# An adapter product moved behind a chunk's gate half, with its loads reordered, in an FFN kernel on one core

## Chip, cores and metric

The kernel runs on one core of a Trainium2 chip. The metric is the device time of one execution in microseconds (us). Before the change the median of four runs is 474.83 us, from 474.81 to 474.93.

A core has engines that run side by side, each with its own instruction stream: TensorE (PE in the profile, its weight loads PEld), VectorE (DVE), ScalarE (ACT), GpSimd (POOL) and SyncE (SP), which here only issues transfers. They wait for one another through semaphores.

## What is computed

Each of 8 batches of x (256 rows of 1024) goes through a low-rank adapter chosen by its id, then through a gated FFN whose activations are rounded to fp8, and is added to x:

```python
# x: (8, 256, 1024); per batch one adapter: B (16 x 1024), A (1024 x 16)
Bx  = einsum('bni,bri->bnr', x, B[ids])
c   = einsum('bnr,bor->bno', Bx, A[ids])
gate = fq(c) @ gate_w.T          # gate_w, up_w: (2752, 1024)
up   = fq(c) @ up_w.T            # fq: to fp8 and back, with a scale
hidden = silu(gate) * up
out  = x + fq(hidden) @ down_w.T # down_w: (1024, 2752)
```

## The kernel before

The 2048 tokens are four blocks t = 0..3 of 512, two batches each. Everything is held transposed, tokens along the free dimension. A block has three steps: B's product (`bx`, 64 small matmuls), A's product (`c`), whose result is rounded to fp8 into `xg[t]`, and the big products. The 2752 hidden rows are 22 chunks c of 128 (the last has 64). For a chunk and a block, `gate_up(c, t)` makes 16 matmuls of 128x512 into two PSUM tiles `y`: eight (k = 0..7) for the gate, j = 0, and eight for the up half, j = 1. ACT takes the silu (L702), DVE multiplies and rounds to `hid` (L731). After all chunks the down projection runs (`yd`) and the result goes out.

The first NFIRST = 5 chunks are held in SBUF, and the blocks enter one after another while their inputs still arrive: block 0 with chunks 0 to 4, block 1 with chunks 0 to 2, then chunks 3 and 4 of block 1 with the adapter products of blocks 2 and 3 between them. From chunk 5 on, all four blocks take each chunk (L780 to L785).

Block 1's adapter is the part in question. `block_1` (L765) is called between steps 11 and 12 of `gate_up(4, 0)`. It first writes DVE's half of the split of A (`split`, L448: two instructions, L454 and L455, that write into `a_parts[0]`, for A's rows held twice, the rounded value in the one copy and what rounding leaves over in the other; POOL does the other half of the columns at L473, as early as A has landed). Then `two_times_b_in_parts` (L585) issues the 64 matmuls on x's block 1 and B, and takes the result apart: a rounded part `bm_parts` (L597, one half by DVE, one by ACT), what is left, `rest` (L600, DVE), and a copy of each to the other partitions (L608, ACT). After the four matmuls that remain of chunk 4, `two_times_a_parts` (L659) makes c of the two halves of the columns: for each, 8 matmuls on bm_parts and 8 on rest, into four PSUM tiles, which ACT and DVE round to xg (L614, L616). Then `gate_up(0, 1)` begins.

PE's instructions are issued in the order in which they are written (`multiply`, L524), and so are the DVE and ACT instructions named above. A PSUM tile is one of eight slots that go round.

All loads of this stage are issued by SyncE in the order written, but for a few at the start that ACT issues. Each issue waits until the one eight places before has landed. The order is: x of block 0 in four pieces, with B and A for it between; chunks 0 (in two loads) to 4 (L422); the adapter numbers of six batches read into registers (L424); B for block 1 (two loads of 68 KB); x of block 1, k = 0..6 (L427, 1792 KB); A for block 1 (L431, four loads of 64 KB); x of block 1, k = 7 (L432, 256 KB); x of blocks 2 and 3 (2 MB each) and their B and A. A chunk is 1 MB, 128 rows of 16 blocks of 128; `gate_up_of` (L78) says where, and the host lays out the blocks of a chunk's row in the order h, j, k, where h is the upper or lower half of the eight k (L993). L718 picks the block for (j, k).

```python
        gate_up(NFIRST - 1, 0, between={12: block_1})
        two_times_a_parts(bms[0])
        gate_up(0, 1, turns=(2, 2, 2, 2))
```

With turns=(2, 2, 2, 2), the gate and the up half take turns by two k, so that the first steps need only the first columns of xg.

Of the kernel before, what the change touches and what calls it, by code (L numbers as in the profile page):

```python
# [19 lines left out]
P = 128  # L20
# [6 lines left out]
NH = H // P  # L27
NI = (I + P - 1) // P
# [5 lines left out]
NFIRST = 5  # L34
# [3 lines left out]
KS = NH // 2  # L38
# [9 lines left out]
def rows_of(c):  # L48
    return TAIL if c == NI - 1 else P


def high(ap):

    return ap.bitcast(BF16)[..., 1::2]
# [6 lines left out]
def x_of(x4, t, k):  # L61

    first = 0
    for n in PIECES[t]:
        if k < first + n:
            break
        first += n
    at = (t * NH + first) * P * TB
    piece = x4[at : at + n * P * TB].rearrange("(p k n) -> p k n", p=P, k=n)
    return piece, first  # L70


def x_row(x4, t, k):
    piece, first = x_of(x4, t, k)
    return piece[:, k - first, :]


def gate_up_of(w_gu, c):  # L78
    at = c * 2 * NH * P * P
    return w_gu[at : at + 2 * NH * P * rows_of(c)].rearrange("(p n) -> p n", p=P)  # L80
# [13 lines left out]
def general(  # L94
# [62 lines left out]
    def three_parts(w):  # L157
        parts = [w]
        rows, size = w.shape[0], prod(w.shape[1:])
        for i in range(2):  # L160
            r = shaped(wpool.tile([P, 2 * NH * P], F32, tag=f"r{i}", name=f"g_r{i}"), w)
            nc.vector.tensor_tensor(r, parts[-1], high(parts[-1]), ALU.subtract)
            parts.append(r)
        return parts
# [29 lines left out]
    def gate_up(hid):  # L194
        for c in range(NI):
            n = rows_of(c)
            w = wpool.tile([P, 2 * NH * P], F32, tag="w", name="g_wgu")
            nc.sync.dma_start(out=w[:, : 2 * NH * n], in_=gate_up_of(w_gu, c))
            w = w[:, : 2 * NH * n]

            order = "p (h j k n) -> p h j k n" if n == P else "p (h k j n) -> p h j k n"
            ws = [
                high(part).rearrange(order, h=2, j=2, k=KS) for part in three_parts(w)
            ]
            ps = []
            for j, x in enumerate((xg, xu)):
                y = psum.tile([P, TB], F32, tag="ps", name=f"g_y{j}")[:n]
                terms = [(k, part) for part in ws for k in range(NH)]
                for i, (k, part) in enumerate(terms):
                    nc.tensor.matmul(  # L210
                        y,
                        lhsT=part[:, k // KS, j, k % KS, :],
                        rhs=x[:, k, :],
                        start=(i == 0),
                        stop=(i == len(terms) - 1),
                    )
                ps.append(y)
            g = work.tile([P, TB], F32, tag="g", name="g_g")[:n]
            nc.scalar.activation(g, ps[0], AF.Silu, scale=gate_s[:n])
            v = work.tile([P, TB], F32, tag="v", name="g_v")  # L220
            nc.vector.scalar_tensor_tensor(
                v[:n],
                in0=ps[1],
                scalar=up_by_down[:n],
                in1=g,
                op0=ALU.mult,
                op1=ALU.mult,
            )
            quantize(hid[:n, c, :], v, n)
# [55 lines left out]
def adaln_ffn(  # L285
# [64 lines left out]
    with ExitStack() as fast:  # L350
# [23 lines left out]
        def adapter_of(batch, queue):  # L374
            return queue.value_load(ids_i[0:1, batch : batch + 1], min_val=0, max_val=7)  # L375
# [6 lines left out]
        def load_a_two(t, j, adapter, queue=nc.sync):  # L382
            for g in range(2):
                row = 32 * (2 * g + j) + R * j
                queue.dma_start(
                    out=a_two[t][row : row + R],
                    in_=a8[bass.ds(adapter * 2 * R + g * R, R), :],
                )
# [6 lines left out]
        def load_x(t, k):  # L395
            piece, first = x_of(x4, t, k)
            ks = slice(first, first + piece.shape[1])
            nc.sync.dma_start(out=xs[t][:, ks, :], in_=piece)  # L398

        w_of = {}  # L400

        def load_gate_up(c, parts=1):
            n = NH if c == NI - 1 else 2 * NH
            w = wpool.tile([P, 2 * NH, P], F32, tag="w", name="w_gu")[:, :n]
            src = gate_up_of(w_gu, c).rearrange("p (k n) -> p k n", n=P)
            n //= parts
            for i in range(parts):
                nc.sync.dma_start(out=w[:, bass.ts(i, n)], in_=src[:, bass.ts(i, n)])
            w_of[c] = w

# [6 lines left out]
        load_a_two(0, 0, first, nc.scalar)  # L419
        load_x(0, 7)  # L420
        load_a_two(0, 1, second, nc.sync)
        for c in range(NFIRST):  # L422
            load_gate_up(c, parts=1 if c else 2)
        adapters = [adapter_of(2 + q, nc.sync) for q in range(6)]  # L424
        for j in range(2):
            load_b(b_two[1], j, adapters[j], nc.sync)
        load_x(1, 0)  # L427
        for j in range(2):
            adapter = adapters.pop(0)
            for g in range(2):  # L430
                load_a_twice(a_two[1], 2 * g + j, a8_twice, adapter * 2 + g)  # L431
        load_x(1, 7)  # L432

        for t in (2, 3):
            load_x(t, 0)
# [12 lines left out]
        def split(a, parts, engine):  # L448

            held = tc.keep_in_program_order
            held(engine.tensor_scalar(parts, a, minus, None, ALU.mult))  # L454
            held(engine.tensor_tensor(parts, a, parts.bitcast(F32), ALU.add))  # L455
# [228 lines left out]
        def gate_up(c, t, turns=(NH,), between={}):  # L684


            tail = c == NI - 1
            w = w_of[c]
            cols = bass.ts(t, TB)
            js = range(1 if tail else 2)  # L690
            ys = []
            steps = []
            for i, n in enumerate(turns):
                done = sum(turns[:i])
                steps += product(js, range(done, done + n))
            rows = slice(TAIL, P) if tail else slice(0, P)
            g = work.tile([P, TB], F32, tag="g", name="g")

            def silu():
                gates = ys[0][:TAIL] if tail else ys[0]  # L700
                early(
                    nc.scalar.activation(  # L702
                        g[rows], gates, AF.Silu, scale=gate_s[: gates.shape[0]]
                    )
                )

            def early(instruction):
                if c < NFIRST:
                    tc.keep_in_program_order(instruction)

            for i, (j, k) in enumerate(steps):
                if i in between:
                    between[i]()
                if j == len(ys):
                    ys.append(psum.tile([P, TB], F32, tag="ps", name=f"y{j}"))
                multiply(
                    ys[j],
                    lhsT=high(w[:, k if tail else k // KS * NH + j * KS + k % KS, :]),  # L718
                    rhs=xg[t][:, k, :],
                    start=(k == 0),  # L720
                    stop=(k == NH - 1),
                )
                if j == 0 and k == NH - 1:
                    silu()
            ups = ys[0][TAIL:] if tail else ys[1]
            if tail:
                to = lora.tile([P, 2 * TB], FP8, tag="bm", name="tail", bufs=2)[half_of(t), :TB]
            else:
                to = hid_of(c)[:, cols]
            early(  # L730
                nc.vector.scalar_tensor_tensor(  # L731
                    to,
                    in0=ups,
                    scalar=up_by_down[rows],
                    in1=g[rows],
                    op0=ALU.mult,
                    op1=ALU.mult,
                    saturate=False,
                )
            )  # L740
            if tail:
                nc.vector.tensor_copy(hid_tail[half_of(t), t // 2], to)
            if t == (NTB - 1 if c < NFIRST else 1):
                note_low_bits(w_of[c], P, c)
                if 1 < c <= 1 + 2 * NTB:
                    i, half = divmod(c - 2, 2)
                    ks = slice(half * NH // 2, (half + 1) * NH // 2)
                    note_squares(xg[i][:, ks, :], P, c - 2)
                if c:
                    note_squares(hid[c - 1], P, 2 * NTB + c - 1)  # L750
# [12 lines left out]
        bms = []  # L763

        def block_1():  # L765
            split(a_two[1][:, : H // 4], a_parts[0][:, : H // 4], nc.vector)
            bms.append(two_times_b_in_parts())

        gate_up(NFIRST - 1, 0, between={12: block_1})
        two_times_a_parts(bms[0])  # L770
        gate_up(0, 1, turns=(2, 2, 2, 2))
        for c in range(1, NFIRST - 2):
# [138 lines left out]
    with found_others.Else():  # L911

        k = NH - 1
# [101 lines left out]
```

## Time and profile before

| what | value |
|---|---|
| median of 4 runs | 474.83 us (474.81 to 474.93) |
| the profiled execution | 474.79 us |
| its span in the trace | 473.0 us |
| granted PE clock in the span | 1.0 |
| y matmuls, 128x512 | 1376 |
| chain that ended last: y, yd, c, bx | 63%, 32%, 1%, 1% of the span |
| x for block 0 on that chain | 1% |
| DVE, hid of one chunk and block (L731) | 751 ns |
| DVE, xg (L614) / ACT, xg (L616) | 744 / 688 ns |
| w_gu loads of 1024 KB, median from issue to landing | 4.8 us |
| bytes moved in the span | 53.84 MB, mean 114 GB/s |

The span is what the profile shows of the core; the time of the execution is 1.8 us longer. A row of the timeline gives the start in us, the length in us, the engine, the line of the kernel, the operation, the tile written and the tiles read, the shapes, and how many instructions are merged. In brackets stands the idle time of the engine before it and who ended it. A queue's name with a q (SPq) is an issue of a transfer and not its duration. Matmuls are pipelined: a 128x512 matmul is shown as 379 ns, but the next one starts after 0.22 us.

### The profile page before, as it was taken

To read this page: it belongs to the slowest core of one execution; us is meant where nothing else is said; L and a number is where in the kernel's file an instruction comes from. 1 tells how busy PE (TensorE), PEld (TensorE's weight loads), DVE (VectorE), ACT (ScalarE), POOL (GpSimd) and SP (SyncE) were. 2 spreads that over 40 slices of the span, in tenths; PEclk is the share of its full clock that TensorE was granted. 3 is DMA by queue.
4 is the path that set the end of the run, shared out by engine and by line. 5 is a ranking of instruction groups with operands and counts; after the bars stand their busy time and mean duration, and the time that the engine had idled before them with its cause. 6 is when DMAs were issued, how large, how long until landed. Compare 5 with 4: busy or idle time off the path is not lost.

```text
span 473.0 us, 5972 instructions
## 1 busy us (share of the span) xinstructions
PE 468.3 (99%) x2482; PEld 215.7 (46%) x2482; DVE 106.9 (23%) x168; ACT 193.5 (41%) x252; POOL 11.6 (2%) x26
## 2 busy tenths in 40 slices
PE   8999999999999999999999999999999999999997
PEld 5454544444444444444444444444444444444444
DVE  1342611212121221212122121231120111031031
ACT  1341538996555645443354544359112012021000
POOL 0024200000000000000000000000000000000000
PEclk9999999999999999999999999999999999999999
DMA  8996024322222211222220011133435245153021
GB/s 319 419 387 202 1 91 139 129 89 89 90 89 90 78 25 76 89 90 89 90 73 31 30 62 57 61 101 106 128 123 161 73 178 162 37 207 108 4 114 69
DMA packets 13909, 53.84 MB, mean 114 GB/s; under 512 B 1650, under 2 KB 2930, under 8 KB 10930
## 3 DMA queue, kind: packets, MB, share of 16 engines
q1 hardware_dynamic: 13664, 53.25, 32.3%
q8 instruction: 21, 0.34, 0.3%
q10 hardware_dynamic: 210, 0.14, 0.1%
q14 instruction: 14, 0.11, 0.1%
HBM read 44.99 MB, written 8.39 MB: 113 GB/s over the span
## 4 chain that ended last, share of the span: by engine, by line
PE 97%; DMA 1%; SPq 0%; DVE 0%; issue 0%
PE y L525 63%; PE yd L525 32%; PE c L525 1%; PE bx L525 1%; DMA x<-x 1%; DMA ids_i<-ids 0%; DVE xg L614 0%; SPq L375 0%; PE warm L525 0%; SPq L398 0%; SPq L378 0%; DVE o L822 0%; PE count L525 0%
## 5 line engine op out<-in xcount | busy, mean ns | idle before, releaser
L525 PE MATMUL y<-xg,w_gu 128*128 128x512 fp8e4 x1376 | 298.1, 379 | 0.4 <-DVE xg L614 0.4
L525 PEld LDWEIGHTS <-w_gu 128*128 128x128 bf16 x1376 | 134.0, 98 | 162.7 <-issue 0.6
L525 PE MATMUL yd<-hid,w_d 128*128 128x512 fp8e4 (+2 forms) x693 | 146.0, 373 | 0.0
L702 ACT ACTIVATE g<-y,gate_s 128x512 f32<-128x512 f32 (+1 forms) x88 | 59.7, 682 | 141.1 <-PE y L525 141.0
L731 DVE SCALAR_TENSOR_TENSOR hid<-y,up_by_down,g 128x512 fp8e4<-128x512 f32 x84 | 63.1, 751 | 217.4 <-PE y L525 153.7
L525 PEld LDWEIGHTS <-w_d 128*128 128x128 bf16 x693 | 66.6, 98 | 78.9 <-issue 1.7
L511 ACT ACTIVATE junk<-w_d 128x1408 bf16<-128x1408 uint16 (+1 forms) x16 | 21.2, 1323 | 88.5 <-DMA w_d<-w_d 88.4
L822 DVE SCALAR_TENSOR_TENSOR o<-yd,down_s,x 128x512 f32<-128x512 f32 x28 | 20.0, 747 | 107.3 <-PE yd L525 95.1
L511 ACT ACTIVATE junk<-w_gu 128x2048 bf16<-128x2048 uint16 (+1 forms) x22 | 41.0, 1863 | 0.0
L518 ACT ACTIVATE junk<-hid 128x2048 bf16<-128x2048 fp8e4 x21 | 40.0, 1906 | 0.5
L518 ACT ACTIVATE junk<-xg 128x2048 bf16<-128x2048 fp8e4 x8 | 15.3, 1910 | 0.3
L614 DVE TENSOR_SCALAR xg<-c,inv 128x512 fp8e4<-128x512 f32 x16 | 10.9, 744 | 4.7 <-PE c L525 4.7
L616 ACT ACTIVATE xg<-c,inv 128x512 fp8e4<-128x512 f32 x16 | 9.7, 688 | 1.7 <-PE c L525 1.7
L525 PE MATMUL warm<-zeros 128*128 128x512 bf16 (+1 forms) x27 | 6.5, 400 | 1.2 <-DVE zeros L312 1.2
L822 DVE SCALAR_TENSOR_TENSOR o<-yd,down_s,xg 128x512 f32<-128x512 f32 (+2 forms) x5 | 3.2, 644 | 12.4 <-PE yd L525 9.8
L525 PEld LDWEIGHTS <-zeros 128*128 128x128 bf16 x27 | 2.6, 116 | 4.6 <-issue 2.9
L511 ACT ACTIVATION_READ_ACCUMULATOR junk<-w_gu 128x1 f32 x22 | 4.2, 192 | 0.0
L525 PE MATMUL yd<-hid_tail,w_dt 64*128 64x512 bf16 (+1 forms) x32 | 4.2, 377 | 0.0
L731 DVE SCALAR_TENSOR_TENSOR tail<-y,up_by_down,g 64x512 fp8e4<-64x512 f32 x4 | 3.0, 756 | 4.9 <-ACT g L702 4.8
L518 ACT ACTIVATION_READ_ACCUMULATOR junk<-hid 128x1 f32 x21 | 3.9, 187 | 0.0
L525 PE MATMUL bx<-x,b_four_twice 128*32 128x256 f32 x64 | 3.7, 380 | 0.0
L578 ACT COPY bm<-bx 64x128 f32<-64x128 f32 x2 | 0.5, 262 | 7.1 <-PE bx L525 7.1
(69 smaller groups left out, 56.3 us busy)
## 6 DMA issues: line engine op xcount, KB each, us to landing
w_gu<-w_gu SPq DMA_DIRECT2D x20, 1024.0 KB, 4.8
outT<-o SPq DMA_DIRECT2D x31, 256.0 KB, 2.2
w_d<-w_d SPq DMA_DIRECT2D x8, 704.0 KB, 5.0
w_d<-w_d SPq DMA_DIRECT2D x8, 640.0 KB, 3.8
x<-x SPq DMA_DIRECT2D x2, 2048.0 KB, 12.2
x<-x SPq DMA_DIRECT2D x1, 1792.0 KB, 13.1
w_gu<-w_gu SPq DMA_DIRECT2D x3, 512.0 KB, 4.0
x<-x SPq DMA_DIRECT2D x2, 512.0 KB, 4.0
```

What stands on the lines that cost most here:

```text
L511: nc.scalar.activation(junk_like(w), low(w), AF.Copy, accum_out=lows[:rows, column : column + 1])
L518: nc.scalar.activation(junk_like(q), q, AF.Square, accum_out=squares[:rows, column : column + 1])
L525: tc.keep_in_program_order(nc.tensor.matmul(*args, **kwargs))
L578: copy(bm[64 * to : 64 * (to + 1), other], bx[half][64 * half : 64 * (half + 1)],)
L614: nc.vector.tensor_scalar(to, c, scale, None, ALU.mult, saturate=False)
L616: nc.scalar.activation(to, c, AF.Copy, scale=scale, saturate=False)
L702: nc.scalar.activation(g[rows], gates, AF.Silu, scale=gate_s[: gates.shape[0]])
L731: nc.vector.scalar_tensor_tensor(to, in0=ups, scalar=up_by_down[rows], in1=g[rows], op0=ALU.mult, op1=ALU.mult, saturate=False,)
L822: nc.vector.scalar_tensor_tensor(o, in0=y, scalar=down_s, in1=x, op0=ALU.mult, op1=ALU.add)
```

## The change

Block 1's product is issued between steps 7 and 8 of `gate_up(4, 0)`, that is between chunk 4's gate and its up half, and no longer after the fourth up matmul. In `block_1` DVE's half of A's split comes after the product's rounding and rests. Chunk 4 is laid out in the order j, h, k (all of the gate's blocks first) and loaded in two loads of 512 KB: the gate half at its old place, the up half (`ups_of_last`) behind x of block 1, whose last piece (k = 7) now follows the first directly. A for block 1 comes after the up half. The functions `order_of` and `row_of` carry the layout to the places that read chunk 4.

```diff
+def order_of(c):
+    return "h k j" if c == NI - 1 else "j h k" if c == NFIRST - 1 else "h j k"
+
+def row_of(c, j, k):
+    if c == NI - 1:
+        return k
+    return j * NH + k if c == NFIRST - 1 else k // KS * NH + j * KS + k % KS
...
-        def load_gate_up(c, parts=1):
+        def load_gate_up(c, parts=1, later=()):
...
+            w_of[c] = w
             n //= parts
-            for i in range(parts):
+
+            def load(i):
                 nc.sync.dma_start(out=w[:, bass.ts(i, n)], in_=src[:, bass.ts(i, n)])
-            w_of[c] = w
+
+            for i in range(parts - len(later)):
+                load(i)
+            return [lambda i=i: load(i) for i in later]
...
-        for c in range(NFIRST):
+        for c in range(NFIRST - 1):
             load_gate_up(c, parts=1 if c else 2)
+        ups_of_last = load_gate_up(NFIRST - 1, parts=2, later=(1,))
         adapters = [adapter_of(2 + q, nc.sync) for q in range(6)]
         for j in range(2):
             load_b(b_two[1], j, adapters[j], nc.sync)
-        load_x(1, 0)
+        for k in (0, 7):
+            load_x(1, k)
+        for load in ups_of_last:
+            load()
         for j in range(2):
             adapter = adapters.pop(0)
             for g in range(2):
                 load_a_twice(a_two[1], 2 * g + j, a8_twice, adapter * 2 + g)
-        load_x(1, 7)
...
-                    lhsT=high(w[:, k if tail else k // KS * NH + j * KS + k % KS, :]),
+                    lhsT=high(w[:, row_of(c, j, k), :]),
...
         def block_1():
+            bms.append(two_times_b_in_parts())
             split(a_two[1][:, : H // 4], a_parts[0][:, : H // 4], nc.vector)
-            bms.append(two_times_b_in_parts())
-
-        gate_up(NFIRST - 1, 0, between={12: block_1})
+
+        gate_up(NFIRST - 1, 0, between={8: block_1})
...
-                .transpose(0, 2, 1, 3, 4)
+                .transpose(0, *((1, 2) if c == NFIRST - 1 else (2, 1)), 3, 4)
```

More of the change, by code (lines that the diff above doesn't have):

```diff
@@ L199, in gate_up @@
             w = w[:, : 2 * NH * n]
-            order = "p (h j k n) -> p h j k n" if n == P else "p (h k j n) -> p h j k n"
+            order = f"p ({order_of(c)} n) -> p h j k n"
             ws = [
```

## The prediction

> **What bounds the kernel now.** First I read the page: who holds the chain that ends last, and how much of the span TensorE (PE) is busy.
>
> ```profile
> span 473.0 us, 5972 instructions
> PE 468.3 (99%) x2482; PEld 215.7 (46%) x2482; DVE 106.9 (23%) x168; ACT 193.5 (41%) x252; POOL 11.6 (2%) x26
> PE 97%; DMA 1%; SPq 0%; DVE 0%; issue 0%
> ```
>
> PE is busy for 468.3 of 473.0 us and holds 97% of the chain. The change adds and removes no matmul, so all it can give is idle PE time near the edit. The windows of 5 us show where that is: none from 10 to 30 us and none from 35 to 55 us, but 4.58 of 5.00 busy here:
>
> ```profile
> 30.00:35.00 5.00, 4.58 (x74) 2.69 (x65) 4.31 (x10) 3.41 (x9) 1.61 (x2) 1.00 1.01 410
> ```
>
> (The columns are PE, PEld, DVE, ACT and POOL busy, then the granted PE clock, 1.00, the DMA share and GB/s.) The timeline from 28 to 34.2 us shows what happens there; each row is start, length, engine, line:
>
> ```profile
> 28.87 1.96 PE L525 MATMUL bx<-x,b_twice 128*32 128x128 f32 x64
> 29.74 0.35 DVE L454 TENSOR_SCALAR a_parts<-a,minus 128x256 fp32r<-128x256 f32 x1 [2.52 <-DMA a<-a_twice]
> 29.82 1.07 POOL L454 TENSOR_SCALAR a_parts<-a,minus 128x256 fp32r<-128x256 f32 x1 [5.37 <-DMA a<-a_twice]
> 30.12 0.58 DVE L455 TENSOR_TENSOR a_parts<-a,a_parts 128x256 fp32r<-128x256 f32 x1
> 30.76 1.04 PE L525 MATMUL y<-xg,w_gu 128*128 128x512 fp8e4 x4
> 30.86 0.28 DVE L597 CAST bm_parts<-bx 64x128 fp32r<-64x128 f32 x1 [0.16 <-PE bx L525]
> 30.97 0.72 POOL L455 TENSOR_TENSOR a_parts<-a,a_parts 128x256 fp32r<-128x256 f32 x1
> 31.18 0.61 DVE L600 TENSOR_TENSOR rest<-bx,bm_parts 64x128 fp32r<-64x128 f32 x2
> 31.73 0.66 PE L525 MATMUL c<-bm_parts,a_parts 32*128 32x256 f32 x8
> 31.74 0.61 ACT L608 CAST rest<-rest 64x128 fp32r<-64x128 f32 x2
> 32.40 0.51 PE L525 MATMUL c<-rest,a_parts 32*128 32x256 f32 x8
> 32.97 1.41 DVE L614 TENSOR_SCALAR xg<-c,inv 128x512 fp8e4<-128x512 f32 x2 [0.39 <-PE c L525]
> 33.78 0.61 PE L525 MATMUL y<-xg,w_gu 128*128 128x512 fp8e4 x2 [0.40 <-DVE xg L614]
> ```
>
> The reader is to see a chain with too little behind it. B's product ends at 30.8. DVE and ACT turn it into a rounded part and a rest (until 32.35), and only four y matmuls (30.76 to 31.64) stand before A's product c. The c on bm_parts start at 31.73, those on rest only at 32.40. DVE's first xg follows at 32.97, and 0.81 later the next y, at 33.78. Last, SyncE's issues, which tell when the transfers land:
>
> ```profile
> 15.42 0.43 SPq L398 DMA_DIRECT2D x<-x  x1
> 16.06 4.88 SPq L391 DMA_DIRECT2D a<-a_twice  x4
> 23.18 0.83 SPq L398 DMA_DIRECT2D x<-x  x2
> ```
>
> The page's list of issues gives the 1792 KB piece of x 13.1 us to landing: 15.42 + 13.1 = 28.5. POOL and DVE start the split when A has landed, 29.7. The last 256 KB of x must be in by the product's k = 7, 28.87 + 56 x 0.0295 = 30.52, since its 64 matmuls run at an even step (1.89 us / 64).
>
> **The change part by part.** The sum is made in the profiled execution (474.79 us; span 473.0). The median of the runs shown, 474.83, is 0.04 above it.
>
> *B's product four y earlier.* A y step is 0.2185 us (16.64 us / 76). The product starts at 28.87 - 4 x 0.2185 = 28.00 and the following y at 30.76 - 0.87 = 29.89. PE's amount of work until c is unchanged, so without a stall c would again start at 31.73. What changes is the cover: eight y, 1.75 us, instead of four.
>
> *Rounding and rest.* DVE and ACT follow the product as before, 0.87 earlier: DVE's cast 29.99, its two rests 30.31 to 30.92, ACT's copies of the rest until 32.35 - 0.87 = 31.48. All of it lies behind the eight y. Before, the c on rest waited: behind c at 31.73 they could have started 0.34 later (the A product at 49.67 has its rest part at 50.01), 32.07, and started at 32.40. So 0.33 us is removed, and the shorter c phase may give some more, 0.44 in all (below).
>
> *Split behind the rests.* Its two DVE instructions cost 0.35 + 0.58 and 0.03 between them, 0.96 us. Before, they were done at 30.70 under the product. Now they run 30.94 to 31.90, if A is there. All c of the first half need them. DVE's end to PE's start takes 0.07 (the first xg, 0.744 long, ends at 33.71; y starts 33.78): c at 31.97 instead of 31.73. That gives 0.24 of the gain back. Bounds: not under 0.80 (0.35 plus 0.42, the L670 subtraction of 128x256 from PSUM, plus 0.03); above, it could stand until POOL's half of the split is through (priced in the rivals). I take 0.96, which is this very pair with POOL running beside it.
>
> What is queued behind the split on DVE: the hid of chunk 4, 31.92 to 32.67 instead of 31.84 to 32.59. Then xg, which must not start before 32.67; it has 0.10 to spare. A slot of the second half's c waits for that hid too, as before.
>
> *From c to the next y.* In the unstalled A product of blocks 2 and 3, c starts at 49.67 and DVE's first xg at 50.47: 0.80. Block 1's own rows give 32.97 - 31.73 - 0.33 = 0.91. I take 0.80, the same shapes without a stall: xg at 32.77, y at 32.77 + 0.81 = 33.58 instead of 33.78, a gain of 0.20 us (0.09 with 0.91).
>
> *Loads.* Chunk 4's up half (512 KB) goes behind x, A behind that. At 420 GB/s (the windows between 10 and 25 us show 419 to 428) 512 KB are 1.25 us and 256 KB 0.62. The order on SyncE's queue holds in the trace (chunk 4 in by about 23.2, B 23.4, x 28.5, A 29.7), so:
> - chunk 4's gate by about 21.9, needed at 12.30 + 64 x 0.2185 = 26.3. B for POOL's copies at 22.2 instead of 23.4.
> - x 27.25, needed 28.00; its last piece 27.9, needed 28.00 + 1.65 = 29.65.
> - the up half 29.1, needed 29.89.
> - A 0.62 to 1.2 behind the up half (its bytes; 29.7 - 28.5 before): 29.7 to 30.3. DVE wants it at 30.94. POOL's pair needs 1.87 us (29.82 to 31.69), so it ends between 31.7 and 32.3; the second half's c start at 31.97 + 0.57 = 32.5.
>
> So each load has 0.6 us or more of cover, and POOL's half 0.2. If a cover is gone, PE waits the missing time one to one. The extra issue costs SyncE 0.43 us while transfers are still queued, with the six reads of adapter numbers behind it as before; each issue waits for the one eight places earlier, and the new places wait for chunks 1 to 3, the gate half and B, all landed by 22.9, so the 2 MB of block 2's x still goes out near 23.2. The layout of chunk 4 changes addresses alone: the same matmuls.
>
> *Whether the 0.20 lasts.* Later POOL results stand on transfers that keep their place: b_four's copies end at 43.28 and are wanted at 44.24 - 0.20; a_four's parts end at 47.4 and are wanted at 49.67 - 0.20. Behind that PE is the chain to the end. Sum: 474.79 - 0.20 = 474.59; on the median, 474.63.
>
> A rule speaks against the split's new place. The Trainium skill, "SBUF — State Buffer", section "Who interferes with whom", says that a DVE instruction with two SBUF inputs and a GpSimd instruction that reads SBUF shut each other out for a whole instruction. The row: DVE's L455 ran from 30.12 to 30.70, inside POOL's L454 (29.82 to 30.89). By the rule the split could end as late as in the second rival below, by the row it is the 0.96 used here; the row decides.
>
> **The rivals.**
> 1. *Full cover.* The split ends by 31.66, so c starts at 31.73, xg at 32.53 and y at 33.34: 0.44 us gained, 474.39. For it: POOL may be further on with its pair than before. Against: DVE would have to do the split in 0.72, below both bounds' rows.
> 2. *Split held until POOL is through (slower).* Place: DVE, L454/L455 of block 1. POOL's pair starts 0.1 behind A (29.8 to 30.4) and ends 31.7 to 32.3; then DVE's 0.96, c 0.07 and y 1.61 later: 34.3 to 34.9 against 33.78, so 475.4 to 475.95. It decides against the change once the split ends after 33.78 - 1.61 - 0.07 = 32.10, and by over 0.2% from 33.05. A late A does the same from a landing at 31.1. For it: POOL's instruction took 1.07 where its 512-column form (1.57) suggests 0.8. Against: DVE's pair ended before POOL's first one.
> 3. *The move gains nothing in the transfers.* If x lands at 28.5 as before, the product stands 0.5 us from 28.00 and all behind it: 474.63 + 0.5 = 475.13. Against: 512 KB less ahead of it, and the issue order says it is less.
> 4. *The change doesn't reach PE.* Then the time is 474.83. Against: the order of instructions on PE does show four y moved behind the product.
>
> **How the numbers follow.** Forecast 0.62; full cover 0.09; held split or late A 0.14 (0.04 of it beyond 0.2%); x late 0.05 (0.01 beyond); no reach 0.04; something unnamed 0.03 on each side. A measurement of this kernel tells about 0.2%, 0.95 us, from no change: below 473.88 or above 475.78. The idle PE time near the edit is 0.42, so a gain beyond 0.2% has no row. Faster 0.03; same 0.62 + 0.09 + 0.10 + 0.04 + 0.04 = 0.89; slower 0.08. The range, 474.35 to 475.05, holds the forecast and full cover (474.39), no reach, and the short forms of the held split and the late x; it leaves out about 0.15.
>
> **What would show it.** The product at 28.0 without a wait; DVE's split from about 30.9 to 31.9, and c behind it waiting for DVE at about 31.97 and not for ACT; rest's c without a stall; y at about 33.6. Wrong: PE waiting for x at 28.0 or for chunk 4's weights at 29.9, a split that starts late on A or takes well over 1 us, or c's second half waiting for POOL.

## The result, and the profile after

The changed kernel takes 475.62 us (median), the kernel before 474.83 in the same comparison; the ratio is 1.0019, with a 95% interval of 1.0013 to 1.0025. So it became slower by about 0.8 us, where a gain of 0.20 was predicted. The profiled execution took 475.41 us, 0.62 more than that of before.

First the page of the kernel after: span, busy time and the chain that ended last.

```profile
span 473.6 us, 5972 instructions
PE 467.8 (99%) x2482; PEld 215.5 (46%) x2482; DVE 106.8 (23%) x168; ACT 193.5 (41%) x252; POOL 11.6 (2%) x26
PE 96%; DMA 2%; ACTq 0%; ACT 0%; DVE 0%; issue 0%
```

PE has the same 2482 matmuls and was busy for no longer, 467.8 against 468.3. So the span's added 0.6 us is time without PE. The window of the edit is not where it lies (columns as before: PE, PEld, DVE, ACT, POOL, clock, DMA share, GB/s):

```profile
30.00:35.00 5.00, 4.75 (x51) 2.61 (x48) 4.64 (x10) 3.63 (x9) 1.76 (x2) 1.00 1.00 406
```

PE's busy time in these 5 us rose from 4.58 to 4.75, at the same granted clock. The timeline of the kernel after shows the steps one by one (start, length, engine, line; in brackets the idle time before and who ended it):

```profile
28.07 1.96 PE L544 MATMUL bx<-x,b_twice 128*32 128x128 f32 x64
29.95 1.90 PE L544 MATMUL y<-xg,w_gu 128*128 128x512 fp8e4 x8
30.37 0.61 DVE L619 TENSOR_TENSOR rest<-bx,bm_parts 64x128 fp32r<-64x128 f32 x2
30.59 1.03 POOL L473 TENSOR_SCALAR a_parts<-a,minus 128x256 fp32r<-128x256 f32 x1 [7.29 <-DVE bm_parts L616]
31.02 0.35 DVE L473 TENSOR_SCALAR a_parts<-a,minus 128x256 fp32r<-128x256 f32 x1
31.40 0.43 DVE L474 TENSOR_TENSOR a_parts<-a,a_parts 128x256 fp32r<-128x256 f32 x1
31.70 0.74 POOL L474 TENSOR_TENSOR a_parts<-a,a_parts 128x256 fp32r<-128x256 f32 x1
31.97 0.51 PE L544 MATMUL c<-bm_parts,a_parts 32*128 32x256 f32 x8
32.29 0.43 PE L544 MATMUL c<-rest,a_parts 32*128 32x256 f32 x8
32.75 2.73 DVE L633 TENSOR_SCALAR xg<-c,inv 128x512 fp8e4<-128x512 f32 x4
33.56 2.76 PE L544 MATMUL y<-xg,w_gu 128*128 128x512 fp8e4 x12
```

The stage went as it was drawn up: the product at 28.07, c at 31.97, its second set right behind the first (before it waited until 32.40), the next y at 33.56 against 33.78. And the lead lasts: the last matmul ends at 469.87 us, before it was 470.09; in both profiles that is 436.31 us behind this y. Yet the span ends 0.6 later. What lies behind the last matmul is one DVE instruction, the last store of outT, and the program's closing code. There SyncE waits for the transfers. The waits of SyncE's own queue, from 465 us to the end, first before, then after (who waited for whom, us in total, times, longest):

```profile
SPq L1010 <- DMA outT<-o: 0.2, 1, 0.2
```

```profile
SPq L1029 <- DMA outT<-o: 1.0, 1, 1.0
```

The longer wait doesn't come from a slower store: it landed 2.01 us behind the last matmul's end (471.88), before 2.00 (472.09). What moved is *where in a list* it is waited for. A transfer signals its landing on one of eight semaphores, which take turns. The closing code waits for the eight in one order, the same in every profile of this case. These are SyncE's instructions in a window of the closing line (engine, operation, count; durations in ns; first and last start), before, up to 472.0, when the last store hadn't landed (472.09), then after, from 0.07 behind its landing (471.88):

```profile
L1010 SPq EVENT_SEMAPHORE  x7: 17/28/28, 471.1 to 471.9; - x7
```

```profile
L1029 SPq EVENT_SEMAPHORE  x7: 28/28/28, 472.0 to 472.7; - x7
L1029 SPq DRAIN  x1: 13/13/13, 472.8 to 472.8; - x1
```

Before, the last store had the eighth semaphore. Seven waits ran from 471.10 to 471.88 while it was in flight; one stood behind its landing, and SyncE's drain came 0.10 us later (472.19). After, it has the first. The list stands still until 471.88, then all seven others run one by one: the drain comes at 472.80, 0.92 behind the landing. So the landing is 0.21 us earlier and the list 0.82 longer, 0.61 in all; the spans differ by 0.6. What follows the drain takes 0.8 us in both.

Why the turn moved is in the diff: chunk 4 is loaded in two transfers instead of one. The kernel before issues 104 transfers, 13 times eight, and the kernel after 105. Every transfer behind the added one, up to the last store 450 us on, is on the next semaphore.

### The profile page after: what moved, and what is told of

Read it like the earlier page. It is cut to its first block, busy times and chain, and to the rows that moved or that the text cites. A ratio compares the mean times of both kernels' runs of the same rounds, so it can differ in the third digit from the quotient of the medians.

```text
span 473.6 us, 5972 instructions
## 1 busy us (share of the span) xinstructions
PE 467.8 (99%) x2482; PEld 215.5 (46%) x2482; DVE 106.8 (23%) x168; ACT 193.5 (41%) x252; POOL 11.6 (2%) x26
## 4 chain that ended last, share of the span: by engine, by line
PE 96%; DMA 2%; ACTq 0%; ACT 0%; DVE 0%; issue 0%
PE y L544 62%; PE yd L544 32%; DMA w_gu<-w_gu 1%; PE bx L544 1%; DMA a<-a 1%; PE c L544 1%; ACT L321 0%; DVE xg L633 0%; ACTq L396 0%; ACTq L320 0%; ACTq L389 0%; DVE o L841 0%; ACTq L386 0%; PE count L544 0%
```

## The experiments

Two theories were tried. *T, the turn*: one more transfer puts the last store on the first semaphore, and that costs some 0.8 us at the end, whatever the extra transfer is and wherever it is issued. Its rivals: the loss lies in the moved stage and its loads, and an extra transfer elsewhere costs nothing; or every extra transfer costs, whatever its turn. *S, the split*: DVE's half of the split, now beside POOL's, is held up in a part of the executions, which the one profile of the kernel after doesn't show. All comparisons are medians beside the kernel before on the same chip.

**One and eight small transfers more, in the kernel before.** Each reads the 32 bytes of ids once more, at chunk 12, into a spare tile (n = 1 and n = 8):

```diff
             load_gate_up(c)
+            for i in range(n if c == 12 else 0):
+                spare = const.tile([1, NB], I32, name=f"spare{i}")
+                nc.sync.dma_start(out=spare, in_=ids)
```

> The kernel before with one small transfer more (32 bytes of ids into a tile nobody reads, in a quiet stretch at chunk 12). Nothing of block 1 is touched. Theory T (the last store's place among SyncE's eight turns): the last store of the output falls on the first of the eight semaphores that SyncE waits for at the end, so the other waits come behind its landing: 0.6 to 0.9 us slower than before, 475.4 to 475.7, and in the trace the list of waits starts when the last store has landed and takes about 0.9 us. Theory R1 (the moved loads and the product cost it in the stage of block 1): as before, 474.8. Theory R2 (one more transfer or more instructions cost by themselves): slower too, and then eight more cost as much or more.

> The kernel before with eight small transfers more at the same point, which puts the last store on the same turn as before. T: as before, 474.7 to 474.95. R1: as before too. R2: slower by 0.6 us or more, 475.4 or above.

One more: 475.76 against 474.92, ratio 1.0016 (1.0007 to 1.0025), 0.84 slower. Eight more: 474.90 against 474.92, 0.9997 (0.9988 to 1.0006). One transfer of 32 bytes at a place where nothing waits for it costs the whole loss of the change; eight of them cost nothing, because the turn is the old one again. Both rivals fall. SyncE's closing instructions behind the landing, with one more (landed 472.57), then with eight more (landed 472.69):

```profile
L1013 SPq EVENT_SEMAPHORE  x8: 17/28/28, 472.6 to 473.4; - x8
L1013 SPq DRAIN  x2: 7/10/13, 473.5 to 473.6; - x2
```

```profile
L1013 SPq DRAIN  x2: 7/10/13, 472.8 to 472.8; - x2
L1013 SPq EVENT_SEMAPHORE  x1: 28/28/28, 472.7 to 472.7; - x1
```

Eight waits behind the landing in the one, one in the other.

**Four more.** The same edit with n = 4 puts the last store on the fourth semaphore.

> The kernel before with four small transfers more: the last store falls on the fourth of the eight semaphores in SyncE's closing list, so four waits stand behind its landing. T (each wait behind the landing costs about 0.08 us): 0.25 to 0.4 us slower than before, 475.1 to 475.3; with the 0.4 us gap that the list shows once (between its fourth and fifth wait in the changed kernel) behind the landing too, up to 0.75 slower. If only the first place costs: as before.

475.15 against 474.86, ratio 1.0008 (0.9999 to 1.0017). Landed at 472.20, and then:

```profile
L1013 SPq EVENT_SEMAPHORE  x5: 28/28/28, 472.2 to 472.5; - x5
L1013 SPq DRAIN  x1: 13/13/13, 472.5 to 472.5; - x1
```

The drain is at 472.53, 0.33 behind the landing, so 0.23 more than before; the medians differ by 0.29. The interval alone wouldn't exclude nothing, the list shows it.

**Seven more, in the kernel after.** With the change's own extra transfer that makes eight (the edit above with n = 7 in the changed kernel).

> The changed kernel with seven small transfers more at chunk 12, eight more than before in all, so the last store is on the turn it had before. T: the loss at the end is gone and the 0.2 us of the earlier y stay: 474.5 to 474.7, 0.1 to 0.25 us faster than before. R1 and R2: 475.4 to 475.8, as the changed kernel. If the stage of block 1 loses time in many runs and the profiled one hid it, the runs spread as widely as those of the changed kernel (475.2 to 476.4).

474.71 against 474.92, ratio 0.9994 (0.9985 to 1.0003): the loss is gone, and the last store's landing has one wait behind it again. But the single executions lie apart, six from 474.36 to 474.71 and five from 474.88 to 475.50, and the profiled one (475.25) shows a held split. Its timeline:

```profile
30.47 0.93 POOL L473 TENSOR_SCALAR a_parts<-a,minus 128x256 fp32r<-128x256 f32 x1 [7.64 <-DVE bm_parts L616]
30.96 0.59 DVE L473 TENSOR_SCALAR a_parts<-a,minus 128x256 fp32r<-128x256 f32 x1
31.49 0.72 POOL L474 TENSOR_TENSOR a_parts<-a,a_parts 128x256 fp32r<-128x256 f32 x1
31.59 0.91 DVE L474 TENSOR_TENSOR a_parts<-a,a_parts 128x256 fp32r<-128x256 f32 x1
32.64 0.51 PE L544 MATMUL c<-bm_parts,a_parts 32*128 32x256 f32 x8 [0.83 <-DVE a_parts L474]
34.23 1.25 PE L544 MATMUL y<-xg,w_gu 128*128 128x512 fp8e4 x5 [0.16 <-DVE xg L633]
```

The same two DVE instructions take 1.53 us instead of 0.81. POOL's subtraction began 0.10 before DVE's (31.49, 31.59), and DVE's ended only at 32.49, 0.28 behind POOL's end. PE waited 0.83 us for it, and y came at 34.23 instead of 33.56. (The bracket of POOL's first row names DVE's cast as what it waited for, but A had landed only 0.25 before, at 30.22; where A lands earlier, in the last kernel below, POOL starts without that cast.) In the kernel after's own profile DVE's subtraction began first (31.40, POOL's 31.70) and took 0.43.

**x of block 1 in one load.** This too gives the last store its old turn, by one transfer less. The x that is added at the end is read as if block 1's k = 7 still lay by itself, so the x added to the last 128 features of block 1 comes from a wrong place.

```diff
-PIECES = ((2, 3, 2, 1), (7, 1), (NH,), (NH,))
+PIECES = ((2, 3, 2, 1), (NH,), (NH,), (NH,))
...
-        for k in (0, 7):
-            load_x(1, k)
+        load_x(1, 0)
```

> The changed kernel with x of block 1 in one load of 2 MB instead of 1792 and 256 KB, so the number of transfers is that of before, with none added. x is whole at about 27.8 us and the product wants it at 28.0. T: 474.5 to 474.8, y after the product's stage at about 33.6 as in the changed kernel, or up to 0.3 later if the product has to wait for x. R1 and R2: R2 says as T here, R1 says 475.4 to 475.8.

475.13 against 474.92, ratio 1.0002 (0.9993 to 1.0011), above the 474.5 to 474.8 expected. Again no loss from the turn (the drain comes 0.10 behind the landing); but in the profiled execution the product waits for the whole of x, which landed at 28.68, and the split is held:

```profile
28.82 1.96 PE L543 MATMUL bx<-x,b_twice 128*32 128x128 f32 x64 [0.22 <-DMA x<-x]
31.75 0.58 DVE L472 TENSOR_SCALAR a_parts<-a,minus 128x256 fp32r<-128x256 f32 x1
32.37 0.91 DVE L473 TENSOR_TENSOR a_parts<-a,a_parts 128x256 fp32r<-128x256 f32 x1
```

**The split, alone.** Three kernels have the old turn (seven more transfers) and one part changed. The first leaves POOL's half of the split out: zeros stand in that half of the columns of A's parts for block 1. The second makes POOL's half wait until DVE is ready to start, by a factor (`late`) that DVE copies first. The third puts DVE's split ahead of the product's rounding again.

```diff
# first
-        split(a_two[1][:, H // 4 :], a_parts[0][:, H // 4 :], nc.gpsimd)
+        nc.gpsimd.memset(a_parts[0][:, H // 4 :].bitcast(F32), 0.0)
# second, in block_1; POOL's later work moves behind it
+            late = const.tile([P, 1], F32, name="late")
+            tc.keep_in_program_order(nc.vector.tensor_copy(late, minus))
+            split(a_two[1][:, H // 4 :], a_parts[0][:, H // 4 :], nc.gpsimd, late)
             split(a_two[1][:, : H // 4], a_parts[0][:, : H // 4], nc.vector)
# third, in block_1
-            bms.append(two_times_b_in_parts())
             split(a_two[1][:, : H // 4], a_parts[0][:, : H // 4], nc.vector)
+            bms.append(two_times_b_in_parts())
```

> The changed kernel with seven transfers more (so the last store has its old turn), and POOL's half of the split of A for block 1 replaced by a memset that reads nothing: the second half of that A is zero, so half of block 1's adapter result is left out. Theory S (in many runs DVE's half of the split is held up by POOL's half beside it): DVE's two instructions take 0.8 us or less, c starts at about 31.9 and y at 33.5; the runs lose their upper group, median 474.4 to 474.6. Rival L (the upper group comes from loads that land late, for block 0 or 1): the runs spread as without this edit, 474.4 to 475.5, median near 474.7.

> The changed kernel with seven transfers more, and POOL's half of the split tied to a one-element copy on DVE behind the rests, so that DVE's half starts first (POOL's work for blocks 2 and 3 comes behind it as before). S: DVE's split takes 0.8 to 1.0 us in every run; POOL's half ends at about 32.8, so c's second half waits some 0.3 us, y at 33.6 to 33.75; no upper group, median 474.5 to 474.75. L: the spread stays, and the later POOL costs 0.1 to 0.3 on top.

> The changed kernel with seven transfers more, and DVE's half of the split ahead of the product's rounding again, as before the change; A still lands at about 30.2. The split then runs 30.4 to 31.3 with DVE's cast and rests behind it: rests until 32.2, ACT's copies until 32.8, c on rest at about 32.8 and y at 34.2 to 34.4, so 0.6 to 0.8 us slower than the changed order where that is not held up: 475.1 to 475.4. If the order on DVE doesn't matter: 474.7.

Against 474.86: without POOL's half 474.60 (0.9996, 0.9987 to 1.0005), with POOL late 474.82 (0.9997, 0.9988 to 1.0006; 474.5 to 474.75 was expected), with the split first 475.29 (1.0008, 0.9999 to 1.0017). Without POOL the pair is free, and ten of eleven executions lie between 474.34 and 474.88. That doesn't show that POOL made the upper group of the kernel with seven more. The kernel before, where the pair lies ahead of the product's rounding, also had 15 of its 33 executions at 475.04 or above in that comparison, and 8 of 33 in this one; and chunk 12 in eight loads, below, has POOL's half in place and ten of eleven executions at 474.89 or less. What shows the hold is the rows of the split:

```profile
30.80 0.35 DVE L473 TENSOR_SCALAR a_parts<-a,minus 128x256 fp32r<-128x256 f32 x1
31.19 0.42 DVE L474 TENSOR_TENSOR a_parts<-a,a_parts 128x256 fp32r<-128x256 f32 x1
```

With POOL behind DVE, DVE's subtraction runs wholly inside POOL's first instruction and takes 0.58 instead of 0.91. c comes 4.1 behind the product (27.95 to 32.07), where it is 3.9 with a free pair (28.07 to 31.97 in the kernel after), and that takes most of the stage's gain. c's second half then waits for POOL, but that costs the next y nothing: it comes 1.59 behind c's start in both.

```profile
31.15 0.95 POOL L473 TENSOR_SCALAR a_parts<-a,late 128x256 fp32r<-128x256 f32 x1 [7.80 <-DVE late L783]
31.35 0.58 DVE L474 TENSOR_TENSOR a_parts<-a,a_parts 128x256 fp32r<-128x256 f32 x1
32.98 0.51 PE L540 MATMUL c<-bm_parts,a_parts 32*128 32x256 f32 x8 [0.16 <-POOL a_parts L474]
```

With the split first, DVE starts it when A lands, and the product's rounding stands behind it until 31.61 and the rests until 32.53; c on rest starts at 32.91 and the next y at 34.29. That is 0.7 later than with a free pair in the change's order (33.56), but no later than with a held one (34.23). So with A landing this late the change's order is the better one only where its pair is free.

**Two versions that might keep the gain.** Chunk 12 in eight loads gives the old turn without a spare transfer. In the second, A goes ahead of the last quarter of chunk 4's up half, so that POOL should be through when DVE starts; chunks 12 to 14 in 4, 2 and 2 loads keep the turn.

```diff
# first
+            load_gate_up(c, parts=8 if c == 12 else 1)
# second
+        ups_of_last = load_gate_up(NFIRST - 1, parts=4, later=(2, 3))
...
+        ups_of_last[0]()
         for j in range(2):
             adapter = adapters.pop(0)
             for g in range(2):
                 load_a_twice(a_two[1], 2 * g + j, a8_twice, adapter * 2 + g)
+        ups_of_last[1]()
```

> The changed kernel with chunk 12, which is loaded far ahead of its use, in eight loads of 128 KB instead of one of 1 MB: seven transfers more without any that is useless, and the last store has the turn it had before the change. T: nothing stands behind its landing but the last wait; where DVE's split is not held 474.4 to 474.6, where it is held 475.0 to 475.5, median 474.5 to 474.8. If the seven useless transfers of the earlier run were what helped: 475.5.

> The changed kernel with chunk 4 in four loads, A for block 1 between the two quarters of the up half, and chunks 12 to 14 in eight loads for three, so the last store keeps its turn. A lands 0.6 us earlier, about 29.6; POOL's half runs 29.85 to 31.5 and is nearly over when DVE's subtraction starts at 31.4. S: DVE's split takes 0.8 to 1.0 us in all runs, y at 33.5 to 33.65, no upper group; median 474.4 to 474.65, faster than both kernels. The last quarter lands at about 30.3 and is wanted at 30.8. Rival: DVE is held up by POOL's second instruction instead of its first and nothing is gained (474.7 to 475.2), or PE waits for the last quarter (a row of PE's waits on the weights at 30.8).

Against 474.79: the first 474.74 (1.0001, 0.9992 to 1.001), the second 475.00 (1.001, 1.0001 to 1.0019). The first takes the change's loss away and is even with the kernel before; the profiled execution has a free split (0.35 and 0.43) and y at 33.59. The second missed its aim. A landed 0.9 us earlier, but that put POOL's *second* instruction in DVE's way:

```profile
30.77 0.72 POOL L474 TENSOR_TENSOR a_parts<-a,a_parts 128x256 fp32r<-128x256 f32 x1
30.92 0.72 DVE L473 TENSOR_SCALAR a_parts<-a,minus 128x256 fp32r<-128x256 f32 x1
31.68 0.42 DVE L474 TENSOR_TENSOR a_parts<-a,a_parts 128x256 fp32r<-128x256 f32 x1
32.25 0.51 PE L544 MATMUL c<-bm_parts,a_parts 32*128 32x256 f32 x8 [0.49 <-DVE a_parts L474]
```

DVE's first instruction ended 0.15 behind POOL's (31.65, 31.50), and PE waited 0.49. None of the versions beats the kernel before by more than its interval.

The closing lists side by side, worked out from the events of each profiled execution (us):

| kernel | semaphore of the last store | last matmul ends | it lands | drain | drain behind landing |
|---|---|---|---|---|---|
| before | 8th | 470.09 | 472.09 | 472.19 | 0.10 |
| before, eight more | 8th | 470.69 | 472.69 | 472.77 | 0.08 |
| after, chunk 12 in eight | 8th | 469.90 | 471.90 | 471.98 | 0.08 |
| before, four more | 4th | 470.17 | 472.20 | 472.53 | 0.33 |
| after | 1st | 469.87 | 471.88 | 472.80 | 0.92 |
| before, one more | 1st | 470.56 | 472.57 | 473.50 | 0.93 |

## Why the prediction was wrong

**The step that failed: "Behind that PE is the chain to the end. Sum: 474.79 - 0.20".** The sum carried the gain from the next y straight to the end of the span and priced nothing at the end. The extra load was priced as an issue, "0.43 us while transfers are still queued", and with the places eight before that its neighbours wait for. The same eight turns decide which semaphore the last store has, and that term was left out. It measured 0.82 us (0.92 - 0.10), and four other kernels show it apart from the stage: one small transfer more in the kernel before makes the loss, eight make none, and seven more or chunk 12 in eight loads take it out of the kernel after.

**The split's 0.96 was no one number.** "The row decides" was half right. In the profile after, the pair took 0.81. But in two other profiles of the changed order (seven more, x in one load) it took 1.53 and 1.52, and in the first, where nothing else differs, the stage is 0.7 us longer for it. This is the second rival's mechanism, at its place; it was given 0.14, together with a late A. It isn't what made the loss in the profile after, where the pair was free. How many executions have it wasn't measured. Before, the row that decided (DVE's L455 inside POOL's L454) was one in which DVE had started first; the change makes DVE start after POOL, and that was not weighed.

**The sum of what was found**: -0.21 at the last landing and +0.82 of the list give 475.40 for the profiled execution's 475.41. The medians differ by 0.79; what is left to that from 0.61, 0.18, could come from executions with a held split (0.7 each) or from the landings at the start, which no run tells apart.

**What was right.** The product at 28.07 (28.00), the y behind it at 29.95 (29.89), the split 31.02 to 31.83 (30.94 to 31.90), c at 31.97 (31.97) waiting for DVE and not for rest, xg at 32.75 (32.77), y at 33.56 (33.58). The loads as well: x 26.88 (27.25), its last piece 27.82 (27.9), the up half 29.33 (29.1), A 30.33 (30.3 at the latest). That c came at 31.97 on the dot is in part luck: the product was 0.07 late, the split 0.15 shorter than its 0.96, and c started 0.15 behind the split's end instead of 0.07.

**The stage gained more than forecast, 0.28 and not 0.20.** Block 0's first y came at 12.15 instead of 12.30, but that was lost again at the seventeenth y, the first of chunk 1, where PE's weight loads waited for the chunk to land. Before, then after:

```profile
15.81 1.41 PEld L525 LDWEIGHTS <-w_gu 128*128 128x128 bf16 x8 [0.38 <-DMA w_gu<-w_gu]
```

```profile
15.87 1.41 PEld L544 LDWEIGHTS <-w_gu 128*128 128x128 bf16 x8 [0.60 <-DMA w_gu<-w_gu]
```

The change touches neither that load nor any issued ahead of it, and over the profiles it landed anywhere from 14.17 to 16.29. So the stage is counted from this y to the first y of block 1, worked out from the events of the profiles (us):

| kernel | chunk 1's first y to block 1's first y | what sets it in the stage |
|---|---|---|
| before; before, one more; before, four more | 17.96; 17.97; 17.95 | the rest's copies |
| before, eight more | 18.36 | the same, and a wait of 0.4 for x |
| after; after, chunk 12 in eight | 17.68; 17.68 | free pair |
| after, seven more, without POOL's half | 17.67 | DVE's pair alone |
| after, seven more, POOL late | 17.89 | DVE's subtraction of 0.58 |
| after, A ahead of the last quarter | 18.06 | DVE's rounding of 0.72 |
| after, seven more | 18.39 | held pair |
| after, seven more, split first | 18.37 | the rest's copies |
| after, x in one load | 18.67 | x, held pair |

From block 1's first y to the end of the last matmul all twelve profiles take 436.31 us, to 0.01. So the stage's gain reaches the end in full, and a held pair turns it into a loss of 0.43 (18.39 against 17.96). Of the 0.28 the last matmul shows only 0.22, because chunk 1's first y was 0.06 late (15.88 against 15.82). The step was mis-sized in two places: from the product to the next y it took 5.49 instead of 5.58, mostly by the shorter split, and the four y moved behind the product take 0.86 and not 0.87 (a step is 0.216 where PE doesn't wait; 16.64 / 76 is 0.2189 and not 0.2185).

**The rivals.** Full cover did not come, and not even without POOL's half: there too c started 3.9 behind the product (27.86 to 31.76), as in the kernel after, where full cover needed 3.73. x did not come late. The change did reach PE.

## What to carry over

In this program one transfer more moved every later one to the next of eight semaphores, and that cost more than the stage gained. Before pricing an edit that changes the *number* of transfers, look at what waits for them in a fixed order, the closing code among them, and at which place the last store stands there. An operation moved to run beside another engine's has no price of its own: look in the trace which of the two started first when the row was taken, and whether the move turns that round. To size a gain in one stage, count from the last wait ahead of it that the edit doesn't touch, not from the program's start. When the busy time falls and the span grows, read the tail behind the last busy instruction first.

## What the runs showed of the hardware

The closing waits cost about 0.07 us each where nothing holds them (472.52, 472.60, 472.66, 472.74 in the kernel after), and in one place of the list, between the fourth and the fifth, stood a gap of 0.39 (472.12 to 472.52). So of the 0.92 behind the landing some 0.3 is this gap. In the kernel before a like gap (471.40 to 471.80, fifth to sixth) and with four more transfers another (471.22 to 471.62, first to second) lay where the last store was still in flight, so nobody paid for it. What makes it is open.

What DVE's half of the split takes depends on where POOL stands in its own half, as these profiles have it:

| DVE's instruction | POOL's, and when it began | DVE took |
|---|---|---|
| rounding (L473) | none | 0.35 |
| rounding | rounding, 0.42 to 0.43 before | 0.35 |
| rounding | rounding, 0.49 to 0.50 before | 0.58 to 0.59 |
| rounding | subtraction, 0.15 before | 0.72 |
| subtraction (L474) | none | 0.42 |
| subtraction | rounding, 0.81 before; subtraction, 0.30 after | 0.43 |
| subtraction | rounding, 0.19 to 0.31 before | 0.58 |
| subtraction | subtraction, 0.10 before | 0.91 |

POOL's start hangs on when A lands. A lead of 0.42 to 0.43 before DVE's rounding went with a free pair (two profiles), one of 0.49 to 0.50 with a held one (two profiles); nothing between was seen. The Trainium skill, "SBUF — State Buffer", section "Who interferes with whom", says that whoever issues first has the shared ports for a whole instruction and the other is blocked. The last row comes near that: blocked for the whole of POOL's instruction, DVE's subtraction would end 0.42 behind POOL's end, and it ended 0.28 behind. The roundings of 0.58 to 0.59 and of 0.72 ended 0.15 behind POOL's, where they take 0.35 alone. The subtraction of 0.58 doesn't agree: there POOL had begun first, and DVE's still ended inside POOL's instruction (31.93, POOL's 32.11). Which of POOL's instructions lets DVE in is open.
